# The last seven products of a gated scan and Hadamard FFN kernel: order of P3 and P7, a second bank for X, and the residual of one half on TensorE

## The chip, the cores and the metric

The kernel runs on one core of a Trainium2 chip. The metric is the device time of one execution in microseconds (us). Five engines matter: TensorE (PE in the profile; its weight loads are PEld), VectorE (DVE), ScalarE (ACT), GpSimd (POOL) and SyncE (SP), which here only issues transfers. ScalarE and GpSimd issue transfers too. A q behind an engine's name (POOLq, SPq) means its sequencer.

## The reference, cut to what matters

Two residual layers work on x of 4 x 512 x 512 in fp32:

```python
x = x + layernorm(attn(layernorm(x), Wi, Wf, Wg, Wo, gnorm_w))   # gated scan over time
x = x + layernorm(ffn(layernorm(x), W1, W2, W3))
# ffn: hidden = silu(x @ W1.T) * (x @ W3.T); hidden = fwht(hidden); out = hidden @ W2.T
# layernorm(y) = (y - mean(y)) / sqrt(var(y) + eps) over the last axis, of 512
```

The change touches the end of the second layer for the last of the four batches: the last share of `hidden @ W2.T`, its layernorm, and the addition to x.

## The kernel before, in words

The work goes batch by batch. In the FFN of a batch (`ffn_unit`, units m = 0 to 7) a unit makes one slice of the hidden layer, and two units make a part. `ffn_out(b, part)` multiplies a part's hidden slices with the matching rows of W2 (into which the Hadamard transform was folded once, at the beginning) and adds the result to `outs[b]`, called y below. There are four parts, so y is complete after part 3.

Every matrix product is done with one level of a seven-product scheme: the output is cut in 2 x 2 quarters (i, j), seven products P1 to P7 of combined quarters are made, and quarters of the output are sums of them. A quarter has 256 rows, which are two tiles of 128 partitions (t = 0, 1), and 256 columns. Tile t of half i is tile 2i + t of the batch's four. `ORDER` (L33) gives the order of the products and the PSUM bank that each accumulates in: X takes P1, P6, P7 and P4 one after the other, Y takes P2, Z takes P5 and P3. A bank isn't cleared between its products, so each reading of X gives the sum so far. `seven` (L447) makes a list of seven steps: 8 matmuls (L659: two tiles, two units, two weights each), then one VectorE operation of 128 x 512 (L471) that adds the bank to the quarter of y. The next product in the same bank waits for that reading. PSUM has eight banks, handed out in rotation by `bank`.

TensorE and SP run in the order in which the program is written. For VectorE, ScalarE and GpSimd a scheduler orders the operations by priority and by when their inputs are there; `tc.high_priority` and `tc.issue_after` (put behind a named instruction on its engine) steer it. In the steady part of the program, products of `ffn_out` lie in the list `fill` and are put between the products of `ffn_unit`. After the last unit nothing is left beside them: `flush` runs the seven products of part 2 and then the seven of part 3 (`tail`, L1057) in one row.

For that last part `seven` is called with `by_tile`, and `OutputNorm` with `at_once`:

- `quarter` (L331) takes the statistics of a quarter's tile as soon as the quarter is complete: quarter (0,0) after P2, (1,1) after P7, (0,1) after P3, (1,0) after P4. In P4 the bank is added to y tile by tile (L468), and each tile's statistics follow.
- `half` (L337), once per half i: per tile the aggregate of mean and variance (L345), then for both tiles together eps is added (L244), GpSimd takes the power -0.5 (L247), which gives r, and VectorE negates the means (L348, nm).
- ScalarE then subtracts the mean from each tile of y in place (L358), which is called centring here.
- `residual` (L350) on VectorE: x = y * r + x, one operation of 128 x 512 per tile (L352). All four are held back until the last half's scales are made.
- `stores` (L687): four transfers to the output of 256 KB each, three issued by SP and one by ScalarE (L693).

At the end of the program (listed under the line of the launch, L1104) every engine drains, SP waits for the transfers, and all engines meet at closing semaphores that GpSimd leads.

Of the kernel before, what the change touches and what calls it, by code (L numbers as in the profile page):

```python
# [11 lines left out]
F32 = mybir.dt.float32  # L12
AF = mybir.ActivationFunctionType
ALU = mybir.AluOpType
P = 128
EPS = 1e-5
# [28 lines left out]
def kernel(  # L45
# [14 lines left out]
    nc = tc.nc  # L60
    B, T, D = x.shape
    FF = w1.shape[1]
    NT = T // P
# [3 lines left out]
    NU = NF // 2  # L67
    NS = 2
    H = T // 2
    URGENT, SOON = 400, 200  # L70
# [6 lines left out]
    work = ctx.enter_context(tc.tile_pool(name="work", bufs=1))  # L77
    small = ctx.enter_context(tc.tile_pool(name="small", bufs=2))
    psum = ctx.enter_context(tc.tile_pool(name="psum", bufs=8, space=bass.MemoryType.PSUM))
# [8 lines left out]
    def bank(name):  # L88
        return psum.tile([P, 2, H], F32, tag="ps", name=name)
# [13 lines left out]
    acts = deque()  # L103
    scaled = deque()
    sums = deque()
# [25 lines left out]
    xs = {}  # L131
# [88 lines left out]
    ident = const.tile([P, P], F32, tag="ident", name="ident")  # L220
# [4 lines left out]
    power_t = const.tile([P, NT], F32, tag="power", name="power")  # L225
# [12 lines left out]
    def inverse_root(mv, eps, name):  # L238


        n = mv.shape[1]
        r = small.tile([P, n], F32, tag="rs", name=f"rs_{name}", bufs=8)
        if isinstance(eps, float):
            read["rs"] = nc.vector.tensor_scalar(r, mv[:, :, 1], eps, None, ALU.add)  # L244
        else:
            nc.vector.tensor_add(r, mv[:, :, 1], eps)
        read["power"] = nc.gpsimd.tensor_tensor(r, r, power_t[:, 0:n], ALU.pow)  # L247
        return r
# [74 lines left out]
    class OutputNorm:  # L323
# [4 lines left out]
            self.st = small.tile([P, NT, 2, 6], F32, tag="sto", name=f"st_{name}_{b}")  # L328
            self.mv = small.tile([P, NT, 2], F32, tag="mvo", name=f"mv_{name}_{b}")

        def quarter(self, i, j, tiles=(0, 1)):  # L331
            for t in tiles:
                nc.vector.bn_stats(
                    self.st[:, 2 * i + t, j, :], self.y[:, i, t, ts(j, H)]
                )

        def half(self, i, then, at_once=False):  # L337


            b, mv = self.b, self.mv[:, 2 * i : 2 * i + 2]  # L340
            eps = self.eps if isinstance(self.eps, float) else self.eps[b][:, 2 * i : 2 * i + 2]
            name = f"{self.name}_{b}_{i}"
            with tc.high_priority(offset=SOON * i):
                for t in range(2):
                    nc.vector.bn_aggr(mv[:, t, :], self.st[:, 2 * i + t])  # L345
                r = inverse_root(mv, eps, name)
                nm = small.tile([P, 2], F32, tag="nb", name=f"nm_{name}", bufs=8)
                self.last = nc.vector.tensor_scalar(nm, mv[:, :, 0], -1.0, None, ALU.mult)  # L348

            def residual(t):  # L350
                x_t = xs[b][:, 2 * i + t, :]
                nc.vector.scalar_tensor_tensor(  # L352
                    x_t, self.y[:, i, t, :], r[:, t : t + 1], x_t, ALU.mult, ALU.add
                )

            def piece(t):
                y_t = self.y[:, i, t, :]
                nc.scalar.activation(y_t, y_t, AF.Identity, bias=nm[:, t : t + 1])  # L358
                if at_once and t == 0:
                    return  # L360
                for k in range(2) if at_once else (t,):
                    then(partial(residual, k), k)

            for t in range(2):
                if at_once:
                    with tc.high_priority(offset=SOON * i):
                        piece(t)
                else:
                    acts.append(partial(piece, t))

    xts = {}

# [71 lines left out]

    def seven(name, multiply, quarter, done=None, add=False, by_tile=False):  # L447

        ps = {}

        def make(what, a, bb, which, first):
            if first:
                ps[which] = bank(f"{which}_{name}")
            multiply(ps[which], a, bb, first)  # L460
            split = by_tile and what == "P4"
            q = {"P1": (0, 0), "P5": (1, 1), "P6": (0, 1), "P2": (0, 0), "P7": (1, 1),
                 "P3": (0, 1), "P4": (1, 0)}[what]
            to = quarter(*q)
            with tc.high_priority(offset=URGENT):
                if split:
                    for t in range(2):
                        nc.vector.tensor_add(to[:, t], ps[which][:, t], to[:, t])  # L468
                        done(*q, t)
                elif what in ("P2", "P7", "P3") or add:  # L470
                    read[what] = nc.vector.tensor_add(to, ps[which], to)  # L471
                else:
                    read["copy"] = nc.scalar.copy(to, ps[which])  # L473
            if what in ("P2", "P7", "P3", "P4") and done is not None and not split:
                done(*q)
            if what in ("P2", "P7", "P3") and not by_tile:
                while scaled and scaled[0][0] == 0:
                    acts.append(scaled.popleft()[1])
                for entry in scaled:
                    entry[0] -= 1  # L480
                for _ in range(min(pace[what], len(sums))):
                    with tc.issue_after(read[what].ins):
                        sums.popleft()()

        return [partial(make, *step) for step in ORDER]
# [145 lines left out]
    hts, outs = {}, {}  # L631
# [11 lines left out]
    down_w = {}  # L643
# [5 lines left out]
    def ffn_out(b, part):  # L649

        ms = range(part * NS, (part + 1) * NS)
        w = {m: down_w.pop((b, m)) for m in ms}

        def multiply(ps, a, bb, first):
            if b not in outs:
                outs[b] = work.tile([P, 2, 2, D], F32, tag="wide", name=f"f_{b}", bufs=3)
            for t in range(2):
                for m in ms:
                    nc.tensor.matmul(  # L659
                        ps[:, t, :], hts[b, m][:, a, ts(t, P)], w[m][:, W2[bb], :],  # L660
                        start=first and t == 0 and m == ms[0], stop=m == ms[-1],
                        skip_group_check=True,
                    )

        norm = {}

        end = b == B - 1 and ms[-1] == NU - 1
        held = []

        def done(i, j, tile=None):  # L670
            if not norm:
                norm[0] = OutputNorm(b, outs[b], EPS, "f")

            def store(residual, t):
                if not end:
                    sums.append(residual)
                    if t:
                        sums.append(partial(stores, range(2 * i, 2 * i + 2)))
                    return
                held.append(residual)  # L680
                if len(held) == NT:
                    with tc.issue_after(norm[0].last.ins):
                        for make in held:
                            make()
                    stores(range(NT))

            def stores(tiles):  # L687
                for t in tiles:
                    if b < B - 1:
                        eng = nc.gpsimd  # L690
                    else:
                        eng = nc.scalar if t == NT - 2 else nc.sync
                    eng.dma_start(out=out[b, ts(t, P), :], in_=xs[b][:, t, :])  # L693

            if not end:
                sums.append(partial(norm[0].quarter, i, j))
                if j == 1 - i:
                    sums.append(partial(norm[0].half, i, store))
                return
            with tc.high_priority(offset=SOON * i):  # L700
                norm[0].quarter(i, j, (0, 1) if tile is None else (tile,))
            if j == 1 - i and tile != 0:
                norm[0].half(i, store, True)

        return seven(
            f"po_{b}_{part}", multiply, lambda i, j: outs[b][:, i, :, ts(j, H)],
            done if ms[-1] == NU - 1 else None, add=part > 0, by_tile=end,
        )


    def load_wo():
# [177 lines left out]
    first, second = transposes(0, "a")  # L889
# [127 lines left out]
    for b in range(B):  # L1017
        last = b == B - 1
        late = {}
        for m in range(NU):  # L1020
# [8 lines left out]
            if b == 0 and m in LOW:  # L1029
                p, what, k = LOW[m]  # L1030
# [5 lines left out]
            if m and m % NS == 0:  # L1036
                if last and m == NU - NS:
                    fill.extend([None] * 8)
                fill.extend([None] + ffn_out(b, m // NS - 1))
# [14 lines left out]
            pace.update(FULL)  # L1054
            with behind("P7"), tc.high_priority(offset=SOON):
                combine_weights()
        tail = ffn_out(b, NU // NS - 1)  # L1057
        if b == 1:
            load_attn_w(3, 0)
            fill.extend([None] + tail)  # L1060
# [47 lines left out]
```

## Time and profile before

| what | us |
|---|---|
| median of 3 runs (lowest to highest) | 810.37 (810.26 to 810.43) |
| the profiled execution's own time | 810.51 |
| its span, first to last instruction | 808.7 |
| TensorE busy with matmuls (3720 of them) | 797.8 |
| VectorE busy | 496.0 |
| ScalarE busy | 266.3 |
| GpSimd busy | 67.4 |

The busy times are shares of the whole span and say little of its end. For the last 21 us the busy times by stretch are (TensorE's products of part 3; from the last product to the last residual; the rest):

```profile
core 0: us, PE busy (x) PEld busy (x) DVE busy (x) ACT busy (x) POOL busy (x), PEclk, DMA share, GB/s
787.50:799.70 12.20, 12.13 (x57) 10.33 (x55) 7.35 (x16) 0.00 (x0) 0.00 (x0) 1.00 0.00 0
799.70:804.80 5.10, 0.00 (x0) 0.00 (x0) 4.78 (x14) 2.67 (x4) 1.40 (x2) 0.73 0.24 90
804.80:808.70 3.90, 0.00 (x0) 0.00 (x0) 0.00 (x0) 0.00 (x0) 0.00 (x0) 0.50 0.41 153
```

In each row the length of the stretch is followed by the busy time of each engine and its number of instructions; PEclk is the granted TensorE clock as a share of full speed. A time in a timeline is the start in us from the span's start; a group of equal instructions is one line with its count (x2).

### The profile page before, as it was taken

The page shows a single profiled execution, that of the slowest core. Times are in us where ns is not written, and L with a number is a line of the kernel's source. Part 1 is how long each engine was busy: PE and PEld are TensorE (multiplying, and loading weights), DVE is VectorE, ACT ScalarE, POOL GpSimd, SP SyncE. Part 2 cuts the span into 40 slices and gives each one's busy share as a digit, 9 for nine tenths or more (in the row PEclk, how much of TensorE's full clock was granted, in tenths as well). Part 3 has the DMA queues.
Part 4 walks back from the last instruction along what each step waited for, and adds up shares of the span by engine and source line. Part 5 has one row for each costly group of instructions (what it writes and reads, how often), then busy time and mean ns, then how long its engine had stood idle before and what let it go on. Part 6 is the DMA issues. An engine that isn't in the chain of part 4 may idle for free.

```text
span 808.7 us, 9917 instructions
## 1 busy us (share of the span) xinstructions
PE 797.8 (99%) x3720; PEld 693.1 (86%) x3720; DVE 496.0 (61%) x1011; ACT 266.3 (33%) x380; POOL 67.4 (8%) x105
## 2 busy tenths in 40 slices
PE   9999999999999999999999999999999999999995
PEld 7888688888888888888888888888888888888884
DVE  6789888898867964445336458545434544444345
ACT  4373846434334211133222224233331111331111
POOL 2111203002211100001000001000000000100000
PEclk9999999999999999999999999999999999999998
DMA  9997536765879974245663354636374442544201
GB/s 303 397 335 281 178 154 207 229 234 211 299 258 326 286 304 163 112 162 215 235 204 154 129 165 170 246 122 243 113 218 160 160 182 91 206 165 182 85 6 52
DMA packets 66480, 160.63 MB, mean 199 GB/s; under 512 B 4864, under 2 KB 40320, under 8 KB 66432
## 3 DMA queue, kind: packets, MB, share of 16 engines
q1 hardware_dynamic: 57232, 115.69, 41.8%
q0 software_dynamic: 8480, 43.00, 13.7%
q10 hardware_dynamic: 720, 1.31, 0.4%
q8 instruction: 29, 0.48, 0.2%
q14 instruction: 19, 0.16, 0.1%
HBM read 115.94 MB, written 44.04 MB: 198 GB/s over the span
## 4 chain that ended last, share of the span: by engine, by line
PE 96%; DVE 2%; issue 0%; ACT 0%; DVEq 0%; POOL 0%; POOLq 0%
PE X_f L494 27%; PE X_po L659 13%; PE Z_f L494 13%; PE X_a L494 10%; PE Z_po L659 7%; PE Y_f L494 7%; PE Z_a L494 5%; PE X_y L601 3%; PE Y_po L659 3%; PE Y_a L494 3%; PE Z_y L601 2%; PE Y_y L601 1%; PE h L771 1%; PE warm L867 1%; PE h L787 1%; PE pt_a L389 0%
## 5 line engine op out<-in xcount | busy, mean ns | idle before, releaser
L494 PE MATMUL X_f<-xt_f,w 128*128 128x256 f32 x1024 | 242.2, 379 | 0.1
L494 PEld LDWEIGHTS X_f<-xt_f,w 128*128 128x128 f32 x1024 | 194.1, 190 | 27.7 <-DVE d_f L471 0.5
L473 ACT COPY d_f<-X_f 128x512 f32<-128x512 f32 x96 | 56.3, 586 | 329.8 <-PE X_f L494 297.6
L659 PE MATMUL X_po<-w,ht 128*128 128x256 f32 x512 | 120.9, 379 | 0.2 <-DVE f L471 0.2
L494 PE MATMUL Z_f<-xt_f,w 128*128 128x256 f32 x512 | 121.0, 379 | 0.0
L659 PEld LDWEIGHTS X_po<-w,ht 128*128 128x128 f32 x512 | 97.2, 190 | 13.7 <-DVE f L471 0.6
L494 PEld LDWEIGHTS Z_f<-xt_f,w 128*128 128x128 f32 x512 | 97.3, 190 | 13.2
L471 DVE TENSOR_TENSOR f<-X_po,f 128x512 f32<-128x512 f32 x51 | 35.1, 688 | 93.8 <-PE X_po L659 93.7
L509 DVE TENSOR_TENSOR ht<-d_f 128x1024 f32<-128x1024 f32 x32 | 39.2, 1224 | 59.7 <-ACT d_f L635 44.9
L494 PE MATMUL Y_f<-xt_f,w 128*128 128x256 f32 x256 | 60.5, 379 | 0.0
L659 PE MATMUL Z_po<-w,ht 128*128 128x256 f32 x256 | 60.5, 379 | 0.0
L494 PEld LDWEIGHTS Y_f<-xt_f,w 128*128 128x128 f32 x256 | 48.6, 190 | 6.6
L659 PEld LDWEIGHTS Z_po<-w,ht 128*128 128x128 f32 x256 | 48.6, 190 | 6.6
L471 DVE TENSOR_TENSOR d_f<-X_f,d_f 128x512 f32<-128x512 f32 x32 | 22.1, 691 | 49.7 <-PE X_f L494 44.1
L247 POOL TENSOR_TENSOR rs_f<-rs_f,power 128x2 f32<-128x2 f32 x16 | 12.1, 757 | 412.4 <-DVE nm_f L348 347.4
L473 ACT COPY d_a<-X_a 128x512 f32<-128x512 f32 x36 | 21.0, 584 | 67.8 <-PE X_a L494 67.6
L635 ACT ACTIVATE d_f<-d_f 128x1024 f32<-128x1024 f32 x32 | 33.8, 1056 | 1.0
L494 PE MATMUL X_a<-xt_a,wi 128*128 128x256 f32 x128 | 33.0, 380 | 0.1
L494 PE MATMUL X_a<-xt_a,wf 128*128 128x256 f32 x128 | 32.9, 379 | 0.0
L471 DVE TENSOR_TENSOR d_f<-Z_f,d_f 128x512 f32<-128x512 f32 x32 | 22.0, 686 | 16.8 <-PE Z_f L494 16.7
L471 DVE TENSOR_TENSOR f<-Z_po,f 128x512 f32<-128x512 f32 x28 | 19.3, 689 | 19.8 <-PE Z_po L659 19.8
L494 PE MATMUL X_a<-xt_a,wg 128*128 128x256 f32 x128 | 30.4, 381 | 0.0
(168 smaller groups left out, 1016.0 us busy)
## 6 DMA issues: line engine op xcount, KB each, us to landing
w<-s_w SPq DMA_DIRECT2D x72, 896.0 KB, 6.3
s_w<-w POOLq DMA_DIRECT2D x24, 896.0 KB, 6.5
w<-in_W_dram SPq DMA_DIRECT2D x32, 256.0 KB, 5.9
wi<-s_wi SPq DMA_DIRECT2D x6, 896.0 KB, 8.9
wf<-s_wf SPq DMA_DIRECT2D x6, 896.0 KB, 7.0
wg<-s_wg SPq DMA_DIRECT2D x6, 896.0 KB, 5.7
w_h<-w2p POOLq DMA_DIRECT2D x8, 512.0 KB, 6.2
xnd_f<-xn_f POOLq DMA_DIRECT2D x8, 512.0 KB, 6.0
```

The source lines that it names most:

```text
L247: read["power"] = nc.gpsimd.tensor_tensor(r, r, power_t[:, 0:n], ALU.pow)
L471: read[what] = nc.vector.tensor_add(to, ps[which], to)
L473: read["copy"] = nc.scalar.copy(to, ps[which])
L494: nc.tensor.matmul(ps[:, n, :], w[:, a, c, :], xt[:, bb, c, :], start=first and n == 0 and c == 0, stop=c == 1, skip_group_check=True,)
L509: nc.vector.tensor_mul(to.rearrange("p (t k) f -> p k t f", t=2), a.rearrange("p k (t f) -> p k t f", t=2), b2.rearrange("p k (t f) -> p k ...
L601: nc.tensor.matmul(ps[:, t, :], og[:, a, c, ts(t, P)], w[c][:, bb, :], start=first and t == 0 and c == 0, stop=c == 1, skip_group_check=True,)
L635: nc.scalar.activation(d[:, 0], d[:, 0], AF.Silu)
L659: nc.tensor.matmul(ps[:, t, :], hts[b, m][:, a, ts(t, P)], w[m][:, W2[bb], :], start=first and t == 0 and m == ms[0], stop=m == ms[-1], sk ...
L771: nc.tensor.matmul(p, h_sb, t[:, k, :], start=True, stop=True)
L787: nc.tensor.matmul(ps[b][ts(u, Q)], h_sb[ts(b, Q), 0:Q], t[ts(b, Q), 0 if u else 2, :], start=True, stop=True,)
L867: nc.tensor.matmul(p, ident, ident, start=True, stop=True)
```

## The change

`last_out` takes the place of `ffn_out` for the last part of the last batch. The other parts and batches keep their code; what only the last part used (`by_tile`, `at_once`, `held`) leaves `seven`, `OutputNorm` and `ffn_out`.

- The order of the products becomes P1, P2, P5, P6, P3, P7, P4, so P7 and P4, both of bank X, follow each other.
- X has two banks, one per tile, and is added to y tile by tile. All four banks are taken when `last_out` is called, which is before part 2's products are run.
- All of VectorE's operations of the part stand in one fixed chain, in the order of the code.
- First half (tiles 0 and 1): complete after P3. Its r is made in P7's step. ScalarE builds two diagonal matrices from r, TensorE accumulates x (times the identity) and y (times the diagonal) in a bank, four matmuls of 128 x 512 behind P4. ScalarE adds the bias -mean * r while it writes the bank to x, and issues the store of each tile, the second tile's evacuation behind the first one's store.
- Second half (tiles 2 and 3): each tile has its own aggregate, r, power, negated mean and centring. Tile 2's residual is one operation with one store; tile 3's is cut into two halves of 256 columns, with a store each. SP issues these three.

The core of the diff; p1, p2, p5, p6 and p3 do their product and its addition, p2 also the statistics of (0,0):

```diff
+    def last_out(b, part):
...
+        for which in "XYZ":
+            tiles = [bank(f"{which}_end") for _ in range(2 if which == "X" else 1)]
+            ps[which] = [tiles[t % len(tiles)][:, t, :] for t in range(2)], tiles
...
+        def scales(*tiles):
+            k = slice(tiles[0], tiles[-1] + 1)
+            for t in tiles:
+                vector(nc.vector.bn_aggr, mv[:, t, :], st[:, t])
+            vector(nc.vector.tensor_scalar, r[:, k], mv[:, k, 1], EPS, None, ALU.add)
+            nc.gpsimd.tensor_tensor(r[:, k], r[:, k], power_t[:, k], ALU.pow)
+            if tiles[0] > 1:
+                vector(nc.vector.tensor_scalar, nm[:, k], mv[:, k, 0], -1.0, None, ALU.mult)
+                for t in tiles:
+                    y_t = y[:, 1, t - 2, :]
+                    nc.scalar.activation(y_t, y_t, AF.Identity, bias=nm[:, t : t + 1])
...
+        def diagonals():
+            for t in range(2):
+                nc.scalar.activation(diag[:, t], ident, AF.Identity, scale=r[:, t : t + 1])
...
+        def first_half():
+            pr = [psum.tile([P, D], F32, tag="ps", name=f"r_{t}_end") for t in range(2)]
+            for t in range(2):
+                nc.tensor.matmul(pr[t], ident, x_t[:, t, :], start=True, stop=False)
+            for t in range(2):
+                nc.tensor.matmul(pr[t], diag[:, t], y[:, 0, t, :], start=False, stop=True)
+            stored = None
+            for t in range(2):
+                with ExitStack() as order:
+                    if t:
+                        order.enter_context(tc.issue_after(stored.ins))
+                    nc.scalar.activation(
+                        x_t[:, t, :], pr[t], AF.Identity, bias=nm[:, t : t + 1]
+                    )
+                stored = nc.scalar.dma_start(out=out[b, ts(t, P), :], in_=x_t[:, t, :])
+
+        def residual(t, k):
+            x_k = x_t[:, t, k]
+            vector(
+                nc.vector.scalar_tensor_tensor,
+                x_k, y[:, 1, t - 2, k], r[:, t : t + 1], x_k, ALU.mult, ALU.add,
+            )
+            nc.sync.dma_start(out=out[b, ts(t, P), k], in_=x_k)
...
+        def p7():
+            multiply(S3, T3, "X", False)
+            add("X", 1, 1, (0,))
+            stats(0, 1, 0)
+            add("X", 1, 1, (1,))
+            stats(0, 1, 1)
+            scales(0, 1)
+            diagonals()
+            stats(1, 1, 0)
+
+        def p4():
+            multiply(A22, T4, "X", False)
+            add("X", 1, 0, (0,))
+            stats(1, 0, 0)
+            scales(2)
+            stats(1, 1, 1)
+            first_bias()
+            add("X", 1, 0, (1,))
+            stats(1, 0, 1)
+            scales(3)
+            residual(2, slice(0, D))
+            for k in range(2):
+                residual(3, ts(k, H))
+            first_half()
+
+        return [p1, p2, p5, p6, p3, p7, p4]
...
-        tail = ffn_out(b, NU // NS - 1)
+        tail = (last_out if last else ffn_out)(b, NU // NS - 1)
```

More of the change, by code (lines that the diff above doesn't have):

```diff
@@ L329, in __init__, with quarter @@
             self.mv = small.tile([P, NT, 2], F32, tag="mvo", name=f"mv_{name}_{b}")
-        def quarter(self, i, j, tiles=(0, 1)):
-            for t in tiles:
+        def quarter(self, i, j):
+            for t in range(2):
                 nc.vector.bn_stats(
@@ L335, in quarter, with half @@
                 )
-        def half(self, i, then, at_once=False):
+        def half(self, i, then):
             b, mv = self.b, self.mv[:, 2 * i : 2 * i + 2]
@@ L347, in half @@
                 nm = small.tile([P, 2], F32, tag="nb", name=f"nm_{name}", bufs=8)
-                self.last = nc.vector.tensor_scalar(nm, mv[:, :, 0], -1.0, None, ALU.mult)
+                nc.vector.tensor_scalar(nm, mv[:, :, 0], -1.0, None, ALU.mult)
             def residual(t):
@@ L358, in piece @@
                 nc.scalar.activation(y_t, y_t, AF.Identity, bias=nm[:, t : t + 1])
[L359 to L362, printed above, removed]
+                then(partial(residual, t), t)
             for t in range(2):
[L365 to L369, printed above, removed]
+                acts.append(partial(piece, t))
     xts = {}
@@ L443, in transpose_fold, with seven @@
         return [partial(make, h) for h in range(3)]
-    def seven(name, multiply, quarter, done=None, add=False, by_tile=False):
+    def seven(name, multiply, quarter, done=None, add=False):
         ps = {}
@@ L460, in make @@
             multiply(ps[which], a, bb, first)
-            split = by_tile and what == "P4"
             q = {"P1": (0, 0), "P5": (1, 1), "P6": (0, 1), "P2": (0, 0), "P7": (1, 1),
@@ L465, in make @@
             with tc.high_priority(offset=URGENT):
[L466 to L470, printed above, removed]
+                if what in ("P2", "P7", "P3") or add:
                     read[what] = nc.vector.tensor_add(to, ps[which], to)
@@ L473, in make @@
                     read["copy"] = nc.scalar.copy(to, ps[which])
-            if what in ("P2", "P7", "P3", "P4") and done is not None and not split:
+            if what in ("P2", "P7", "P3", "P4") and done is not None:
                 done(*q)
-            if what in ("P2", "P7", "P3") and not by_tile:
+            if what in ("P2", "P7", "P3"):
                 while scaled and scaled[0][0] == 0:
@@ L665, in ffn_out, with done @@
         norm = {}
-        end = b == B - 1 and ms[-1] == NU - 1
-        held = []
-        def done(i, j, tile=None):
+        def done(i, j):
             if not norm:
@@ L674, in store @@
             def store(residual, t):
[L675 to L703, printed above, removed]
+                sums.append(residual)
+                if t:
+                    sums.append(stores)
@@ L705, in ffn_out, with stores @@
+            def stores():
+                for t in range(2 * i, 2 * i + 2):
+                    eng = nc.gpsimd if b < B - 1 else nc.sync
+                    eng.dma_start(out=out[b, ts(t, P), :], in_=xs[b][:, t, :])
+            sums.append(partial(norm[0].quarter, i, j))
+            if j == 1 - i:
+                sums.append(partial(norm[0].half, i, store))
         return seven(
             f"po_{b}_{part}", multiply, lambda i, j: outs[b][:, i, :, ts(j, H)],
-            done if ms[-1] == NU - 1 else None, add=part > 0, by_tile=end,
+            done if ms[-1] == NU - 1 else None, add=part > 0,
@@ L708, in ffn_out, with vector, multiply, add @@
         )
+    def last_out(b, part):
+        ms = range(part * NS, (part + 1) * NS)
+        w = {m: down_w.pop((b, m)) for m in ms}
+        y, x_t = outs[b], xs[b]
+        ps = {}
+        for which in "XYZ":
+            tiles = [bank(f"{which}_end") for _ in range(2 if which == "X" else 1)]
+            ps[which] = [tiles[t % len(tiles)][:, t, :] for t in range(2)], tiles
+        chain = []
+        def vector(op, *args):
+            with ExitStack() as order:
+                if chain:
+                    order.enter_context(tc.issue_after(chain[-1].ins))
+                chain.append(op(*args))
+        def multiply(a, bb, which, first):
+            at, tiles = ps[which]
+            for t in range(2):
+                for m in ms:
+                    nc.tensor.matmul(
+                        at[t], hts[b, m][:, a, ts(t, P)], w[m][:, W2[bb], :],
+                        start=first and m == ms[0] and (t == 0 or len(tiles) > 1),
+                        stop=m == ms[-1], skip_group_check=True,
+                    )
+        def add(which, i, j, tiles=(0, 1)):
+            at, banks = ps[which]
+            if len(banks) > 1:
+                for t in tiles:
+                    to = y[:, i, t, ts(j, H)]
+                    vector(nc.vector.tensor_add, to, at[t], to)
+            else:
+                to = y[:, i, :, ts(j, H)]
+                vector(nc.vector.tensor_add, to, banks[0], to)
+        st = small.tile([P, NT, 2, 6], F32, tag="sto", name="st_end")
+        mv = small.tile([P, NT, 2], F32, tag="mvo", name="mv_end")
+        r = small.tile([P, NT], F32, tag="nb", name="r_end", bufs=8)
+        nm = small.tile([P, NT], F32, tag="nb", name="nm_end", bufs=8)
+        def stats(i, j, t):
+            vector(nc.vector.bn_stats, st[:, 2 * i + t, j, :], y[:, i, t, ts(j, H)])
+        def scales(*tiles):
[6 more added lines that the diff above has]
+                vector(nc.vector.tensor_scalar, nm[:, k], mv[:, k, 0], -1.0, None, ALU.mult)
+                for t in tiles:
+                    y_t = y[:, 1, t - 2, :]
+                    nc.scalar.activation(y_t, y_t, AF.Identity, bias=nm[:, t : t + 1])
+        diag = work.tile([P, 2, P], F32, tag="o", name="diag")
+        def diagonals():
+            for t in range(2):
+                nc.scalar.activation(diag[:, t], ident, AF.Identity, scale=r[:, t : t + 1])
+        def first_bias():
+            vector(
+                nc.vector.scalar_tensor_tensor,
+                nm[:, 0:2], mv[:, 0:2, 0], -1.0, r[:, 0:2], ALU.mult, ALU.mult,
+            )
[3 more added lines that the diff above has]
+                nc.tensor.matmul(pr[t], ident, x_t[:, t, :], start=True, stop=False)
+            for t in range(2):
+                nc.tensor.matmul(pr[t], diag[:, t], y[:, 0, t, :], start=False, stop=True)
+            stored = None
+            for t in range(2):
+                with ExitStack() as order:
+                    if t:
+                        order.enter_context(tc.issue_after(stored.ins))
+                    nc.scalar.activation(
+                        x_t[:, t, :], pr[t], AF.Identity, bias=nm[:, t : t + 1]
+                    )
+                stored = nc.scalar.dma_start(out=out[b, ts(t, P), :], in_=x_t[:, t, :])
+        def residual(t, k):
+            x_k = x_t[:, t, k]
+            vector(
+                nc.vector.scalar_tensor_tensor,
+                x_k, y[:, 1, t - 2, k], r[:, t : t + 1], x_k, ALU.mult, ALU.add,
+            )
+            nc.sync.dma_start(out=out[b, ts(t, P), k], in_=x_k)
+        def p1():
+            multiply(A11, B11, "X", True)
+            add("X", 0, 0)
+        def p2():
+            multiply(A12, B21, "Y", True)
+            add("Y", 0, 0)
+            for t in range(2):
+                stats(0, 0, t)
+        def p5():
+            multiply(S1, T1, "Z", True)
+            add("Z", 1, 1)
+        def p6():
+            multiply(S2, T2, "X", False)
+            add("X", 0, 1)
+        def p3():
+            multiply(S4, B22, "Z", False)
+            add("Z", 0, 1)
+        def p7():
[22 more added lines that the diff above has]
+        return [p1, p2, p5, p6, p3, p7, p4]
```

## The prediction, on record before the changed kernel was run

> **What bounds the kernel now.** I read the page's chain first, then the timeline of the last 25 us, then the instructions of the closing line L1104. The chain says that the kernel is TensorE almost to its end:
>
> ```profile
> PE 96%; DVE 2%; issue 0%; ACT 0%; DVEq 0%; POOL 0%; POOLq 0%
> ```
>
> So nothing but the end is open to this change. The timeline of the end (start, length, engine, line, operation, names, and in brackets the idle time before):
>
> ```profile
> 796.21 0.69 DVE L471 TENSOR_TENSOR f<-X_po,f 128x512 f32<-128x512 f32 x1 [1.03 <-PE X_po L659]
> ...
> 797.74 1.89 PE L659 MATMUL X_po<-w,ht 128*128 128x256 f32 x8
> 797.94 0.69 DVE L471 TENSOR_TENSOR f<-Z_po,f 128x512 f32<-128x512 f32 x1 [0.25 <-PE Z_po L659]
> 798.67 0.75 DVE L333 BATCH_NORM_STATS2 st_f<-f 128x6 f32<-128x256 f32 x2
> 799.34 0.33 DVE L345 BATCH_NORM_AGGREGATE mv_f<-st_f 128x2 f32<-128x12 f32 x2
> ...
> 799.85 0.75 DVE L468 TENSOR_TENSOR f<-X_po,f 128x256 f32<-128x256 f32 x2
> 799.97 1.33 ACT L358 ACTIVATE f<-f,nm_f 128x512 f32<-128x512 f32 x2 [23.24 <-DVE nm_f L348]
> ...
> 801.53 0.17 DVE L244 TENSOR_SCALAR rs_f<-mv_f 128x2 f32<-128x2 f32 x1
> ...
> 801.85 0.69 POOL L247 TENSOR_TENSOR rs_f<-rs_f,power 128x2 f32<-128x2 f32 x1 [1.12 <-DVE nm_f L348]
> 801.98 2.74 DVE L352 SCALAR_TENSOR_TENSOR x<-f,rs_f,x 128x512 f32<-128x512 f32 x4 [0.21 <-issue]
> 802.76 2.32 SPq L693 DMA_DIRECT2D out_dram<-x  x3
> ```
>
> TensorE ends at 799.63 (797.74 + 1.89), VectorE at 804.72, the last store is issued at 804.75 and, at the 2.09 us to landing of these stores, lands at 806.84. Yet the span ends at 808.7. Line L1104, the end of the program, says what stands between (length min/median/max in ns, then first and last start):
>
> ```profile
> L1104 POOLq DRAIN x3: 45/93/6117, 801.8 to 808.4; - x3
> L1104 SPq DRAIN x3: 7/7/7, 807.0 to 808.2; - x3
> ```
>
> GpSimd's drain starts behind its last power and lasts to 807.93, which is 5.39 us after that power ended (802.54). SP is through with its waits for the stores at 807.1, 0.8 us earlier. After the drain 0.77 us of closing semaphores follow. So by this trace the end is held by GpSimd's last power plus 5.39 us, and the stores have 0.8 us to spare. The chain leads through the residuals, since it follows instructions; the drain is a sequencer's.
>
> **What stays.** The seven products keep their 8 matmuls each at 0.216 us (1.73 a product), so TensorE still reaches the last of P4 at 799.63, if nothing stalls. P4 now follows P7 on the same X, which P3 kept apart. The second bank has to cover that: P7's tile 0 (four matmuls from 796.01) ends at 797.04, VectorE's 0.42 us add of it ends at 797.49, and P4's first weight load would start at 797.52. The price of a late read is in part 2 of the same product, where it happened:
>
> ```profile
> 778.64 1.59 PEld L659 LDWEIGHTS X_po<-w,ht 128*128 128x128 f32 x8 [0.57 <-DVE f L471]
> 778.64 1.99 PE L659 MATMUL X_po<-w,ht 128*128 128x256 f32 x8 [0.17 <-DVE f L471]
> ```
>
> The weights went 0.05 us behind the add, and matmuls then caught up 0.1 us. Here they come 0.02 late: no stall. Were both adds needed first (the second ends at 798.36), the stall would be 0.8 us; but VectorE reaches P4's tile 0 only at 799.38, 0.6 after it is there, so 0.2 us of it would show. The four banks are drawn earlier in the rotation than before; the buffer that part 2's Y then gets is read last at 775.64 and written at 776.58: nothing.
>
> **VectorE's row to the last root.** From P7's second tile on (its add can start at 797.94, as that of the product in this place does now) VectorE never waits, so I add its starts. A 256-column add or statistic takes 0.415, and the next independent one starts 0.08 before its end (L468: two in 0.75): 0.33 a step. One that needs the result starts 0.03 after it: 0.45. Aggregates step 0.12 and 0.23, two-column scalings 0.08 if not needed at once. In the new order: add and statistic 0.66, two aggregates to the eps add 0.36, statistics of quarter (1,1) 0.08 + 0.34, so P4's tile 0 is added at 799.38. Its statistic, aggregate, eps add: 0.45 + 0.45 + 0.23. Then negated mean, the other statistic, the first half's bias, which slip in ahead of tile 1: 0.08 + 0.08 + 0.33 + 0.08. Then tile 1: 0.45 + 0.45 + 0.23. The last eps add starts at 797.94 + 4.27 = 802.21 and ends at 802.38; before, both tiles went together and it ended at 801.70. Tile by tile costs the last root 0.68 us, because each tile pays its dependent steps alone.
>
> **The last power.** It follows 0.15 us later (801.70 to 801.85 now): 802.53. It has one column; such powers took 0.547 to 0.563 in the first stage (L247, 128x1), against 0.69 to 0.71 for two. Free of others it ends at 803.08. But tile 2's residual, a 0.75 us operation with both inputs in SBUF, is next on VectorE at 802.37, ahead of the power. How that goes stands at 120 us:
>
> ```profile
> 120.34 0.75 DVE L352 SCALAR_TENSOR_TENSOR x<-y,rs_y,x 128x512 f32<-128x512 f32 x1
> ...
> 120.58 1.06 POOL L247 TENSOR_TENSOR rs_f<-rs_f,power 128x2 f32<-128x2 f32 x1 [24.88 <-DVE rs_f L244]
> 121.01 0.68 DVE L471 TENSOR_TENSOR y<-Y_y,y 128x512 f32<-128x512 f32 x1
> ```
>
> The power took 1.06 instead of 0.71 and ended 0.55 after the residual. The Trainium skill speaks against the change here: "GPSIMD Engine Reference", section Specifications, says that GpSimd shares its SBUF interfaces with VectorE and contends with operations of two SBUF inputs. The nearest row in place, 801.85, shows no hold (0.69 beside a residual), but there the residual started 0.13 after the power. By that row the power ends at 803.08, by the rule and the row at 120 us at 803.12 + 0.41 = 803.53 (0.55 less 0.14 for the missing column). I take the second, since the order of starts is that of 120 us. Before, the last power ended at 802.54: +0.99, or +0.54 without the hold.
>
> **The rest, beside this.** Removed: two 0.74 us residuals on VectorE, two 0.7 us activations of the first half. One two-column power becomes two of one column. Added: two diagonals on ScalarE (128 columns: between 0.20 for one column, L878, and 0.37 for 256, L394; I take 0.3), four 128x512 matmuls, two evacuations at 0.60 (L772), one more store. The first power, 0.7 us from 799.28, runs beside operations with one SBUF input and isn't held; the diagonals are there by 800.8. The matmuls' row is
>
> ```profile
> 15.51 1.02 PE L771 MATMUL h<-w2p,had 128*128 128x512 f32 x2
> ```
>
> two in 1.02, a step of 0.43, 1.7 us for four, behind P4, so ended by 801.6. A rule speaks against this too: "FP8 and Floating Point Precision", TensorE Precision Notes, gives four passes to full fp32, where this step is two of 0.21. By the rule they would end near 803.4. In either case ScalarE evacuates and issues two stores at 0.6 + 0.35 each. If tile 3's centring (0.72) goes ahead of them in its queue, they are issued by 805.0 and land by 807.1; SP would be done by 807.4, still 1.5 us ahead of the drain: worth 0. If the evacuations go ahead of the centring, tile 3's residual waits up to 1 us and lands as late: 0 again. Undisturbed, the residual's halves (0.47 each: 0.745 less 0.275 for 256 columns) end at 804.42, SP issues at 804.45, landing at 806.54 at the same 2.09 us.
>
> **Sum.** Drain to 803.53 + 5.39 = 808.92, + 0.77 = 809.7, against 808.7: +0.99 on the profiled execution (810.51, of which 1.8 lie outside its span), which stands 0.14 above the median. On 810.37 it makes 811.4.
>
> **Rivals.** All figures on the median; within 0.2% (1.62 us) is about what a measurement of this kernel can tell from no change.
> Forecast, power held, drain fixed: 811.4 (811.0 to 811.9), 0.46.
> No hold, the power goes first: 810.9, 0.20. For it: 801.98, where a residual did come second after 0.21 us of unexplained idle time; against it: the other powers that met a running residual or add.
> The drain isn't fixed behind the power but follows the last landing by 1.1 us (806.84 to 807.93 fits equally; one execution can't tell): the end moves with the last store, 806.54 against 806.84, so 810.1, between 809.7 and 810.6 with ScalarE's order; 0.21.
> Slower: the drain works off what GpSimd's powers of the end left behind, 2.7 us for each of today's two. A third makes 811.4 + 2.7 = 814.1. It passes 0.2% once the drain grows by 0.63 us. Against it: users of a power's result start 0.03 after its end, so no backlog is seen; 0.10.
> Faster by over 0.2%: the drain bounds nothing and stores are issued by 803.1: 808.7, 0.03. VectorE's row speaks against it.
>
> **Numbers.** The range leaves out the growing drain and the ends of two others: 809.8 to 812.0. Slower is the growing drain plus 0.02 of the forecast's upper end, faster the last case, the rest is the same.
>
> **What would show it.** In the new trace: TensorE's P4 directly behind P7 with no idle time named; the last eps add near 802.4, the last power at 802.5 and over 0.9 us long; GpSimd's drain again 5.4 us behind it, ending after SP's. A drain that ends about 1.1 us behind the last landing breaks the sum; so does idle time on VectorE between 798 and 802.

## The result and the profile after

| what | before | after |
|---|---|---|
| median, us (20 runs each) | 810.36 | 811.40 |
| lowest to highest | 810.19 to 810.85 | 811.16 to 811.86 |
| the profiled execution's own time | 810.51 | 811.36 |
| its span | 808.7 | 809.6 |

The ratio is 1.0013 (95% interval 1.0007 to 1.0019): 1.04 us longer, which is within 0.2%. The forecast was 811.4.

The chain of waits of the changed kernel is again TensorE's:

```profile
PE 97%; DVE 2%; ACT 0%; issue 0%; POOL 0%; ACTq 0%; DVEq 0%; POOLq 0%
```

The busy times by stretch of its end, over the same three parts of the work (columns as in the table of before):

```profile
787.50:799.50 12.00, 12.00 (x57) 10.57 (x56) 7.58 (x19) 0.00 (x0) 0.40 (x1) 1.00 0.00 1
799.50:804.80 5.30, 3.43 (x8) 1.17 (x7) 4.14 (x15) 3.40 (x6) 1.92 (x3) 1.00 0.18 66
804.80:809.60 4.80, 0.00 (x0) 0.00 (x0) 0.00 (x0) 0.00 (x0) 0.00 (x0) 0.54 0.41 145
```

In the middle part TensorE has new work (8 records, 3.43 us), VectorE 0.6 us less than before, ScalarE 0.7 and GpSimd 0.5 more. But the part in which no engine computes is what grew, from 3.90 to 4.80 us. The timeline says what it starts from:

```profile
797.81 0.42 DVE L699 TENSOR_TENSOR f<-X_end,f 128x256 f32<-128x256 f32 x1
...
799.26 0.41 DVE L699 TENSOR_TENSOR f<-X_end,f 128x256 f32<-128x256 f32 x1
799.33 1.88 PE L756 MATMUL r_end<-x,ident 128*128 128x512 f32 x4
...
800.64 0.55 POOL L734 TENSOR_TENSOR r_end<-r_end,power 128x1 f32<-128x1 f32 x1 [0.83 <-DVE nm_end L699]
...
801.05 1.88 PE L758 MATMUL r_end<-f,diag 128*128 128x512 f32 x4
...
802.09 0.15 DVE L699 TENSOR_SCALAR r_end<-mv_end 128x1 f32<-128x1 f32 x1
...
802.22 0.74 DVE L699 SCALAR_TENSOR_TENSOR x<-f,r_end,x 128x512 f32<-128x512 f32 x1
802.32 1.06 POOL L734 TENSOR_TENSOR r_end<-r_end,power 128x1 f32<-128x1 f32 x1 [1.13 <-DVE nm_end L699]
802.34 0.72 ACT L739 ACTIVATE f<-f,nm_end 128x512 f32<-128x512 f32 x1 [0.96 <-DVE nm_end L699]
...
803.42 0.88 DVE L699 SCALAR_TENSOR_TENSOR x<-f,r_end,x 128x256 f32<-128x256 f32 x2 [0.45 <-POOL r_end L734]
...
804.78 0.35 ACTq L767 DMA_DIRECT2D out_dram<-x  x1
```

The last eps add ends at 802.24. The last power starts 0.10 us after tile 2's residual and takes 1.06 us, where the same one-column operation at 800.64, beside no such residual, took 0.55. The end of the program, line L1220 in this kernel (length min/median/max in ns, then first and last start):

```profile
L1220 POOLq DRAIN  x3: 45/102/6499, 802.3 to 809.3; - x3
L1220 SPq DRAIN  x3: 7/7/7, 807.3 to 809.0; - x3
```

GpSimd's drain (6499 ns; its record begins as the power does, in before too) ends at 808.79, which is 5.40 us after the end of that power at 803.38. In the kernel before it is the same 5.40: the 5.39 of the prediction comes from rounded times. SP is through at 807.4. The last store, ScalarE's second, landed at 807.19: 1.60 us ahead of the drain's end, where it was 1.10 before. A drain that follows the landing should have kept that distance.

The trace of after comes to the last part 0.13 us earlier: its TensorE is that much ahead by 7 us already, in records that the change doesn't touch. Such shifts between executions are taken out below where single times are compared.

### The profile page after: what moved, and what is told of

It is laid out like the page before. It is cut to its first block, busy times and chain, and to the rows that moved or that the text cites. A ratio compares the mean times of both kernels' runs of the same rounds, so it can differ in the third digit from the quotient of the medians.

```text
span 809.6 us, 9941 instructions
## 1 busy us (share of the span) xinstructions
PE 801.1 (99%) x3728; PEld 694.4 (86%) x3728; DVE 495.6 (61%) x1015; ACT 266.7 (33%) x382; POOL 68.3 (8%) x106
## 4 chain that ended last, share of the span: by engine, by line
PE 97%; DVE 2%; ACT 0%; issue 0%; POOL 0%; ACTq 0%; DVEq 0%; POOLq 0%
PE X_f L481 27%; PE Z_f L481 13%; PE X_po L646 13%; PE X_a L481 10%; PE Y_f L481 7%; PE Z_po L646 6%; PE Z_a L481 5%; PE X_y L588 3%; PE Y_po L646 3%; PE Y_a L481 3%; PE Z_y L588 2%; PE Y_y L588 1%; PE X_end L705 1%; PE h L887 1%; PE warm L983 1%; PE h L903 1%
## 5 line engine op out<-in xcount | busy, mean ns | idle before, releaser
L646 PE MATMUL X_po<-w,ht 128*128 128x256 f32 x480 | 113.5, 379 | 0.2 <-DVE f L458 0.2
L646 PEld LDWEIGHTS X_po<-w,ht 128*128 128x128 f32 x480 | 91.1, 190 | 12.9 <-DVE f L458 0.6
L458 DVE TENSOR_TENSOR f<-X_po,f 128x512 f32<-128x512 f32 x48 | 33.0, 688 | 91.5 <-PE X_po L646 91.5
L646 PE MATMUL Z_po<-w,ht 128*128 128x256 f32 x240 | 56.7, 379 | 0.0
L646 PEld LDWEIGHTS Z_po<-w,ht 128*128 128x128 f32 x240 | 45.6, 190 | 6.2
L588 PE MATMUL X_y<-wo,og 128*128 128x256 f32 x128 | 30.2, 379 | 0.0
```

The costliest lines, as they stand in the source:

```text
L588: nc.tensor.matmul(ps[:, t, :], og[:, a, c, ts(t, P)], w[c][:, bb, :], start=first and t == 0 and c == 0, stop=c == 1, skip_group_check=True,)
L646: nc.tensor.matmul(ps[:, t, :], hts[b, m][:, a, ts(t, P)], w[m][:, W2[bb], :], start=first and t == 0 and m == ms[0], stop=m == ms[-1], sk ...
```

## The experiments

The theory from the prediction: the end is GpSimd's last operation, plus a fixed drain of 5.40 us, plus about 0.8 us of closing; the whole 1.0 us is that operation ending later. Its rivals: a drain that follows the stores, and one that grows with GpSimd's work. Times are medians; kernels measured side by side shared a chip and the runs of before, and each is compared with these.

**Without the hold.** Tile 3's two half residuals go ahead of tile 2's, so no residual is running when the power starts.

```diff
             scales(3)
-            residual(2, slice(0, D))
             for k in range(2):
                 residual(3, ts(k, H))
+            residual(2, slice(0, D))
```

> The changed kernel with tile 3's two half residuals ahead of tile 2's residual, so no operation with two SBUF inputs runs when the last power starts. Theory (the end is the last power's end plus 5.40 us of drain plus 0.78): the power takes 0.55 instead of 1.06 and ends near 802.87, the drain ends near 808.27, 0.5 us sooner than in the changed kernel: 810.9. Rival (the drain's end follows the last store's landing): ScalarE's second store stays the last to land, so 811.4 as the changed kernel.

Measured 810.81 (810.63 to 811.04) against 810.43 before, ratio 1.0005 (0.9996 to 1.0013). The last power in the timeline, and the end:

```profile
802.38 0.56 POOL L734 TENSOR_TENSOR r_end<-r_end,power 128x1 f32<-128x1 f32 x1 [1.12 <-DVE nm_end L699]
```

```profile
L1220 POOLq DRAIN  x3: 45/93/5997, 802.3 to 808.9; - x3
L1220 SPq DRAIN  x3: 7/7/7, 808.0 to 808.6; - x3
```

The power starts 0.06 later than in after and takes 0.56 instead of 1.06, and the drain ends at 808.34, again 5.40 behind it. The stores now come 0.7 us later (SP through at 808.1), yet the program is 0.6 us shorter. So the hold was worth about half a microsecond of the 1.04, and it was paid through the drain.

**GpSimd later, without need.** One spare one-column multiply on GpSimd, its result unused, behind the last residual:

```diff
+        spare = small.tile([P, 1], F32, tag="spare", name="spare", bufs=1)
...
                 residual(3, ts(k, H))
+            nc.gpsimd.tensor_tensor(spare, x_t[:, 3, D - 1 : D], power_t[:, 0:1], ALU.mult)
             first_half()
```

> The changed kernel with one more GpSimd operation of one column that reads the last residual's output and whose result nobody uses. Theory (5.40 us of drain behind GpSimd's last operation): it starts near 804.45, ends near 805.0, so the drain ends 1.6 us later than in the changed kernel: 813.0. Rival (the drain follows the stores, or nothing of GpSimd's matters): 811.4, unchanged. Rival (the drain grows with GpSimd's operations of the end, 1.8 us for each of three): 7.2 us of drain, 814.8.

Measured 812.63 (812.33 to 813.09), ratio 1.0026 (1.0017 to 1.0036). The multiply in the timeline, then the end:

```profile
804.27 0.19 POOL L823 TENSOR_TENSOR spare<-x,power 128x1 f32<-128x1 f32 x1 [1.00 <-DVE x L699]
```

```profile
L1222 POOLq DRAIN  x3: 45/93/5627, 804.2 to 810.4; - x3
L1222 SPq DRAIN  x3: 7/7/7, 807.2 to 810.1; - x3
```

The stores are as early as in after, and nothing uses the result, but the end moves with it: the drain ends at 809.87, 5.40 behind the multiply. The expectation had taken the multiply at a power's 0.55; it took 0.19, which is the 0.4 by which the time came out below the expected 813.0. A drain that follows the stores is out.

**More work on GpSimd, early.** Four such multiplies, 791.6 to 792.5, 6.4 us ahead of the first power of the end:

```diff
...
             add("Z", 1, 1)
+            for _ in range(4):
+                nc.gpsimd.tensor_tensor(spare, y[:, 0, 0, 0:1], power_t[:, 0:1], ALU.mult)
```

> The changed kernel with four more one-column GpSimd operations in P5's step, some 8 us before the last power; their result is not used. Theory (drain of fixed length behind the last operation): unchanged, 811.4, drain again 5.40 behind the last power. Rival (the drain works off what each operation leaves behind): seven operations instead of three, the drain 5.4 x 7 / 3 = 12.6, so 818.6.

Measured 811.21 (811.12 to 812.1), ratio 1.0011 (1.0002 to 1.0019). The last power ends at 803.26 and the drain at 808.66: 5.40. A drain that grows with the number of multiplies is out. For powers the changed kernel itself says it: it has three at its end, where before had two, and the drain is 5.40 in both.

**One bank for X, still added tile by tile.**

```diff
-            tiles = [bank(f"{which}_end") for _ in range(2 if which == "X" else 1)]
+            tiles = [bank(f"{which}_end") for _ in range(1)]
...
-            if len(banks) > 1:
+            if which == "X":
```

> The changed kernel with one bank for X instead of two, still read tile by tile. If only the tiles' own readings count: P4 waits for nothing or up to 0.8 us, of which 0.2 shows: 811.4 to 811.6. If readings and products of one bank are kept apart as wholes: both adds of P7 come first (to 798.7), P4 starts 1.1 us late and its tile 0 is added only behind the whole product, 1.5 us later than now: 812.9. The prediction named the first with 0.2.

Measured 813.0 (812.88 to 813.53), ratio 1.0033 (1.002 to 1.0045), the slowest of all. The timeline from P7's end:

```profile
796.55 1.03 PE L705 MATMUL X_end<-w,ht 128*128 128x256 f32 x4
...
797.62 0.42 DVE L699 TENSOR_TENSOR f<-X_end,f 128x256 f32<-128x256 f32 x1 [1.04 <-PE X_end L705]
...
798.29 0.41 DVE L699 TENSOR_TENSOR f<-X_end,f 128x256 f32<-128x256 f32 x1
...
798.75 1.99 PE L705 MATMUL X_end<-w,ht 128*128 128x256 f32 x8 [1.17 <-DVE f L699]
```

The add of tile 0 waits for the whole of P7 (1.04 us named to PE), though its own matmuls had long ended, and P4 waits 1.17 us for both adds. In this program a bank is thus kept apart as a whole between its writer and its reader; whether the chip asks for it or only the scheduler, no run here tells. In after the add of P7's tile 0 starts at 796.95, before P7 ends. The last power ends 1.54 later than in after, and the time is 1.6 longer.

**The old order, P7 ahead of P3**, with all else of after; **and the first half on VectorE**, that is P3 ahead of P7, but centring, two residuals behind the others on VectorE, and stores by SP, instead of diagonals and matmuls. These two, and the next two, shared the runs of before (810.31).

```diff
-        return [p1, p2, p5, p6, p3, p7, p4]
+        return [p1, p2, p5, p6, p7, p3, p4]
```

> The changed kernel with P7 ahead of P3 again; the first half's scales move to P3's step, the statistics of quarter (1,1) to P7's. VectorE's row from 797.8 on holds the same operations in another order, its last eps add comes 0.0 to 0.1 us later: 811.4 to 811.5. Rival (the order is what moved the time, by P4 standing behind P7): back towards 810.4.

```diff
-            diagonals()
+            vector(nc.vector.tensor_scalar, nm[:, 0:2], mv[:, 0:2, 0], -1.0, None, ALU.mult)
+            for t in range(2):
+                y_t = y[:, 0, t, :]
+                nc.scalar.activation(y_t, y_t, AF.Identity, bias=nm[:, t : t + 1])
...
-            first_bias()
...
-            first_half()
+            for t in range(2):
+                vector(
+                    nc.vector.scalar_tensor_tensor,
+                    x_t[:, t, :], y[:, 0, t, :], r[:, t : t + 1], x_t[:, t, :],
+                    ALU.mult, ALU.add,
+                )
+                nc.sync.dma_start(out=out[b, ts(t, P), :], in_=x_t[:, t, :])
```

> The changed kernel with its first half done as before: centred by ScalarE, residual by VectorE, behind the second half's in the chain, stored by SP; no diagonals, no matmuls behind P4. Theory: its stores land near 807.8, SP is done at 808.1, still ahead of GpSimd's drain at 808.8, so TensorE's part in the residual is worth nothing: 811.4. Rival (the first half on TensorE does shorten the end): slower than the changed kernel by the two residuals that VectorE takes back, 1.3 us: 812.7.

The old order measured 811.40 (811.24 to 811.91), ratio 1.0014 (1.0007 to 1.0021): as after. Its last power is 1.06 long too and the drain 5.40. The order of P3 and P7 by itself is worth nothing here: VectorE does the same work in another order, and the last power starts 0.07 us later than in after, when the 0.22 us by which this trace is behind are taken out.

The first half on VectorE measured 811.64 (811.14 to 813.27), ratio 1.0016 (1.0008 to 1.0023). Its TensorE is 0.35 us behind after's from the first stage on, which is not the edit's. The last SP stores in the timeline and the end:

```profile
805.34 0.99 SPq L830 DMA_DIRECT2D out_dram<-x  x2
```

```profile
L1228 POOLq DRAIN  x3: 45/93/6497, 802.6 to 809.6; - x3
L1228 SPq DRAIN  x3: 7/7/7, 808.2 to 809.4; - x3
```

The last store lands at 808.04 and SP is through at 808.2; GpSimd's drain ends at 809.13. Without the 0.35 the landing is at 807.69, 0.50 later than in after, and the drain's end at 808.78, where after has 808.79. So TensorE's residual freed VectorE and brought the last landing forward, and it was worth nothing, because the drain covers both.

**Take the drain away.** If GpSimd's last operation is what ends the program, a root made without GpSimd must uncover the stores behind it. In the kernel before and in after alike: square root by ScalarE, reciprocal by VectorE, for the last part only; a square root ahead of the part brings ScalarE's table in (1.28 us, between 776.5 and 778.7 in these traces). The edit of before (that of after is the same in its own functions, and its evacuations are put behind tile 3's centring):

```diff
+                if at_once:
...
+                    with behind("act"):
+                        read["act"] = nc.scalar.activation(r, mv[:, :, 1], AF.Sqrt, bias=eps_t)
+                    nc.vector.reciprocal(r, r)
+                else:
+                    r = inverse_root(mv, eps, name)
```

> The kernel before with the two inverse roots of its end taken from GpSimd: ScalarE makes the square root (its table is loaded once, in ScalarE's idle time behind the last Silu), VectorE the reciprocal. GpSimd has no work in the last 80 us. Theory (the drain, 5.40 us behind GpSimd's last operation, is the end): the drain is over long before, the end becomes the last store's landing plus SP's 0.27 plus 0.8; the residuals can start near 801.6 and end near 804.4, landing at 806.5, span 807.6, so 809.3, 1.1 us faster than before. Rival (the drain follows the last landing by 1.1 us, as it did before by chance or not): landing at 806.5 gives 810.0.

> The changed kernel with the same substitution for its three roots, and with the first half's evacuations held behind tile 3's centring on ScalarE, the order that they have in the changed kernel. Theory: no GpSimd operation, so the end is the last landing, ScalarE's second store, at 807.1 plus 0.27 plus 0.8: span 808.2, so 809.9 to 810.0, 1.4 us faster than the changed kernel, but slower than the kernel before with the same substitution, since the first half's four matmuls take 3.4 us and end at 802.9. Rival (drain follows the landing by 1.1 to 1.6): 811.0 to 811.4.

Measured: before with the root on ScalarE 810.14 (809.79 to 810.47), ratio 0.9998 (0.9990 to 1.0006), and after with it 810.61 (810.42 to 811.08), ratio 1.0005 (0.9997 to 1.0013). Both miss by 0.6 to 0.8, and the first lies nearer to its rival's 810.0. But no drain stands at its end: GpSimd's is over at 726.4, and the closing semaphores follow SP's last wait (807.6) in it, as they do in the other (808.3). What differs is that TensorE came to the last part late, in the first of them by 0.71 us against before: 0.36 in the first 12 us (the kernels without this edit lie between 0.31 ahead and 0.23 behind there), and 0.35 at 164 us, where a product of the first FFN unit waits for ScalarE's copy in this kernel and did not in before:

```profile
164.45 1.35 PE L507 MATMUL X_f<-xt_f,w 128*128 128x256 f32 x5 [0.34 <-ACT d_f L486]
```

Nothing of the edit is near it. The constant eps had a memset at the program's start, but apart from that, VectorE's operations up to the last part stand in the same order in both kernels. What slips is one of them: the addition that starts at 153.50 in before starts at 154.21, which is 0.36 more than the shift of the first 12 us, and ScalarE's copy is late with it. Both kernels with this memset show that, and none of the other ten; why stays open. So the edit was made again with the memset behind the last unit's P7, in a tile that was there already, so that nothing before 772 us differs:

```diff
+        if last:
+            with behind("P7"):
+                nc.vector.memset(unused_t, EPS)
+            ready = small.tile([P, 2], F32, tag="nb", name="ready", bufs=8)
+            with behind("silu"):
+                read["act"] = nc.scalar.activation(ready[:, 0:1], unused_t, AF.Sqrt)
```

> The kernel before with ScalarE's root at its end, as in the run of that name, but eps is written to a tile in use already, behind the last unit, so nothing ahead of the end differs from the kernel before. In that run TensorE reached the last part 0.71 us later than before, by a loss in the first 165 us that has nothing to do with the end; without it its span of 808.4 becomes 807.7. Theory (no GpSimd operation, so stores set the end): 809.4, 1.0 us faster than before. Rival (the end is held by something else and the run's gain of 0.2 is all there is): 810.1.

> The changed kernel with ScalarE's root, eps written as in the run beside this one. TensorE reached the last part 0.99 us later than in the changed kernel in the earlier run of this; without that its span is 808.1. Theory: 809.9, 1.5 us faster than the changed kernel, and 0.5 slower than the kernel before with the same root, because the end is then ScalarE's second store of the first half, behind 3.4 us of matmuls. Rival (the tile-by-tile end is the better one once GpSimd's drain is gone): 809.4 or less.

Measured side by side (before: 810.56): the kernel before with the late root **809.24** (809.14 to 809.6), ratio 0.9986 (0.9979 to 0.9992); after with it 809.79 (809.7 to 810.33), ratio 0.9992 (0.9984 to 1.0000). The first is shorter than the kernel before and the changed one. Its timeline and its end:

```profile
801.25 1.41 DVE L358 SCALAR_TENSOR_TENSOR x<-f,rs_f,x 128x512 f32<-128x512 f32 x2
...
802.03 2.59 SPq L704 DMA_DIRECT2D out_dram<-x  x3
802.58 0.16 DVE L350 RECIPROCAL rs_f<-rs_f 128x2 f32<-128x2 f32 x1
802.84 1.41 DVE L358 SCALAR_TENSOR_TENSOR x<-f,rs_f,x 128x512 f32<-128x512 f32 x2
```

```profile
L1121 POOLq DRAIN  x3: 45/93/5951, 719.5 to 807.1; - x3
L1121 SPq DRAIN  x3: 7/7/7, 806.5 to 806.8; - x3
```

The drain starts at 719.5, behind GpSimd's last power, now of an earlier stage, and is over by 725.4, 5.39 us after that power, beside the products. Now the last landing (806.34) ends the program: SP is through at 806.6, the span ends 0.8 later. From TensorE's last matmul to the end of the span this takes 8.0 us, where before took 9.1: 1.07 us less, where 1.0 was expected. Another 0.28 us of the profiled execution is a shift of the start as above, so of the 1.32 us between the medians an estimated 1.1 are the drain's. In after with the late root, ScalarE's second store is the last one:

```profile
804.60 0.35 ACTq L779 DMA_DIRECT2D out_dram<-x  x1
```

It lands at 806.96, 0.62 later than the last one of the other kernel, and the medians differ by 0.55. Its other stores have landed by 806.27, so once the drain is gone, the first half by TensorE and ScalarE is the later way, by that much.

## Why the prediction was right, point by point

- **TensorE.** P4 follows P7 with no idle time named and ends at 799.50, the predicted 799.63 less the shift of 0.13. Right; the second bank does cover the read. But the price set on doing without it was wrong: "0.2 us of it would show" supposed that tile 0 of the one bank could still be read early. One bank cost 1.6 us, since the reads wait for the whole product as well.
- **The last root.** Predicted 802.38, measured 802.24 + 0.13 = 802.37, against 801.70. The sum of dependent steps held: 0.67 us for tile by tile.
- **The last power.** Predicted end 803.53, measured 803.38 + 0.13 = 803.51. The hold (end 0.42 after the residual; taken as 0.41) is shown by the first experiment, which puts it at 0.5. So the choice for the row at 120 us and the Trainium skill's "GPSIMD Engine Reference", section Specifications, against the row at 801.85 was right. The trace of before holds more such rows than the one that was read: eight two-column powers there start while a VectorE operation with both inputs in SBUF has 0.2 us or more to run, and each ends 0.54 to 0.58 us after that operation (0.80 to 1.75 us long), while no other takes over 0.72, the one at 800.02 beside an addition that reads PSUM included. Of the 0.97 us by which the power ends later, 0.67 is the root and 0.37 the power (0.51 held, 0.14 less for the missing column); 0.07 came back, since the power now starts 0.08 behind the add and not 0.15.
- **The drain.** Predicted 5.39 behind the power and then 0.77. It was 5.40 in all eight traces whose last part has a GpSimd operation, whatever came before it and whenever the stores landed, and the closing then took 0.77 to 0.79. Both rivals on it have fallen. What the drain does in that time stays open: no view shows it.
- **The matmuls of the first half: wrong.** "two in 1.02, a step of 0.43, 1.7 us for four" was mis-sized by two. Each fp32 matmul of the code stands as two records in the profile, so the row showed one matmul, and the four took from 799.33 to 802.93, 3.6 us. (So the 8 matmuls of a product, as described, are 4 in the code: two tiles and two units. The 3720 matmuls counted in the profile before are records too.) The rule that was weighed and set aside, in "FP8 and Floating Point Precision", TensorE Precision Notes, gave 803.4 and was the nearer to 802.93 + 0.13 = 803.06. The bound on the landing failed with it, by 0.2 us: 807.19 + 0.13 = 807.32, against "land by 807.1". It moved nothing, because the last landing stayed 1.6 us ahead of the drain's end.
- **The evacuations** took 0.67 and 0.69, not 0.60, and the diagonals 0.39, not 0.3: both under the same cover.

As a whole, the change shortened what was not the bound (VectorE's residuals), put the last landing 0.5 us later (807.32 against 806.84) where the drain covered it, and lengthened what was the bound, the way to GpSimd's last operation.

## What to carry to other kernels

Look past the last computing instruction: where the program's end waits for an engine's drain, what counts is when that engine did its last operation, however small, and not when the results are stored. Move such an operation earlier, start it before a large two-input operation of VectorE and not behind one, or give it to another engine; then see which transfer becomes the end. Before a duration is multiplied, count how many records of the profile one instruction of the code makes.

## What the runs showed of the hardware that was not expected

- GpSimd's drain at the end of the program lasts 5.40 us from the end of its last operation, be it a power or a multiply, and runs beside other engines' work when that operation is early (719.5 to 725.4).
- A one-column multiply on GpSimd takes 0.19 us, a power 0.55; a power that starts 0.10 us behind a 0.74 us residual takes 1.06.
- An fp32 matmul of 128x512 takes 0.86 us at a granted clock of 1.00, in two records.
- The two kernels with a one-column memset at the program's start lost 0.35 us at 164 us, and none of the ten others did, although VectorE's order was the same; the cause is open.
